# Layer 1's silu written with tanh in a two-layer Mamba and mixture-of-experts kernel

## The chip, the cores and the metric

The kernel runs on one core of a Trainium2 chip. The metric is device microseconds of one execution; lower is better. The core's engines run their own queues in order and meet through semaphores: TensorE (PE; its weight loads are shown apart as PEld), VectorE (DVE), ScalarE (ACT), GpSimd (POOL) and SyncE (SP), which issues most of the DMAs. ACT evaluates its functions (Silu, Tanh, Exp, Ln) with tables; where the next function needs another table, an instruction ACT_TABLE_LOAD stands in its queue.

## The reference

Two layers, each a mixer and a feed-forward, each with a layer norm before it and one behind it, over 4 sequences ("batches") of 512 tokens with 256 features. Layer 0 is a Mamba-2 block with a gated feed-forward, and a routed mixture of 8 experts. The change touches layer 1 alone. Its mixer, for each of 512 inner channels:

```python
projected = jnp.einsum('bld,cd->blc', hidden_states, in_proj_w)
conv_out = _dw_causal_conv_silu(projected, conv_weight, conv_bias)   # 4 taps, then silu
gate = jax.nn.sigmoid(jnp.einsum('bld,cd->blc', hidden_states, gate_proj_w))
X = conv_out.reshape(batch, seqlen, NHEADS, HEADDIM)
dt = jax.nn.softplus(jnp.einsum('blhp,hp->blh', X, dt_w) + dt_b)
a = jnp.exp(dt[..., None] * A)
u = dt[..., None] * B * X
s = _diag_ssm_scan(a, u)          # s_t = a_t s_(t-1) + u_t
y = C * s + D * X
combined = y.reshape(batch, seqlen, INNER) * gate
```

Its mixture of experts: 8 experts with 128 hidden features of which each token uses two, and a shared expert for all.

```python
scores = jax.nn.sigmoid((xt @ gate.T).astype(jnp.float32))
_, sel = jax.lax.top_k(scores + expert_bias[None, :], TOP_K)
...
h = jax.nn.silu(xb @ w1e.T) * (xb @ w3e.T)      # xb: token times its score
oe = (h @ w2e.T).astype(routed.dtype)
...
hs = jax.nn.silu(xt @ shared_w1.T) * (xt @ shared_w3.T)
out = hs @ shared_w2.T
```

## The kernel before

**Two phases.** The first, to about 870 us, runs layer 0's mixer over the four batches and, beside it, the feed-forward and the experts of the batches behind (`feed_forward`, `experts0_in`, `experts0_out`, `experts0_back`). It uses Silu (L601, 8 times), Exp (L708, 64 times), Ln (L212) and, in the feed-forward, Tanh (L310): layer 0's feed-forward already writes silu as `th = tanh(gp / 2)`, then `th = (th + 1) gp` and `hT = 0.5 th up` on DVE (L310 to L313; L1005 to L1007 for the last batch).

The second phase begins with weights loaded on SP's queue (`weight`, L1024: w1i, w1g, dtw, dtb, w1o and more) and constants made on DVE (L1034 to L1041: An = -exp(A_log), BC = B C times a half, D1 = D times a half). Then eight stages run for each batch. Three finish layer 0's experts for two batches; `last_feed_forward` does layer 0's last feed-forward; four are layer 1:

- `mixer1_in`: layer norm, transposition, then for each of four blocks m of 128 channels a projection into a PSUM bank (`ps("b")`, 2 buffers), the convolution (`conv`: one ACT Identity, L199, and three DVE operations, L201, that read the bank) and Silu in place on X (L1058). Then four gates (Tanh, L1065: (1 + tanh) stands for sigmoid, and the constants take up the half), dt from all four X blocks (L1070, with the weights dtw), softplus (`log1p_exp`: Abs L206, Exp L209, Ln L212, with small DVE operations between), and dt, transposed, to DRAM (`by_row`, L255).
- `mixer1_out`: dt comes back from DRAM to all partitions (db, L1088). For each m: POOL makes dt X (L1092), ACT the decay (Exp, L1093) and D1 X (L1094), DVE the scan (L1097), `uu BC + D1 X` (L1098) and the gate (L1099), PE the output projection (L1102); then norm and residual.
- `experts1_in`: layer norm, transposition, router (Tanh, L1139), top two on DVE (L1142 to L1144), scores s (L1146); then the shared expert's hidden features (`gated`: Silu L1116, product L1117).
- `experts1_out`: for each of four chunks c of 128 tokens two halves of four experts each (`inner`). A half's gate and up products (L1164) go to one tile of two PSUM banks (`ps("dc", 2)`, 2 buffers); ACT takes Silu of each expert's 128x128 block with the token's score as scale (L1169, into sg, tag s2b, 2 buffers), DVE makes up times score times sg (L1172), PE turns the result (L1183) and multiplies it by w2 (L1196); then norm, residual and output.

**What sets the order.** Each stage is a generator that yields estimates: PE time, DVE time, a delay, and in some places a stage that has to come first. The loop at the end (L1223 on) picks by these which stage emits its next part, so that stages of different batches stand interleaved in the program. The framework's scheduler then orders each engine's instructions, sets the waits and gives out the buffers; a tile with a tag takes turns in that tag's buffers with all tiles of the tag. `later` pins an instruction to its place in the program.

Of the kernel before, what the change touches and what calls it, by code (L numbers as in the profile page):

```python
# [8 lines left out]
F32 = mybir.dt.float32  # L9
BF16 = mybir.dt.bfloat16  # L10
I32 = mybir.dt.int32
AF = mybir.ActivationFunctionType
ALU = mybir.AluOpType
# [3 lines left out]
B, L, DM = 4, 512, 256  # L17
P = 128
NC = L // P
# [10 lines left out]
OFF, _o = {}, 0  # L30
# [7 lines left out]
def tile_layers(  # L38
# [27 lines left out]
    V, S, G, T = nc.vector, nc.scalar, nc.gpsimd, nc.tensor  # L66
# [4 lines left out]
    small = ctx.enter_context(tc.tile_pool(name="small", bufs=2))  # L71
# [18 lines left out]
    col = base.tile([P, NCOL], F32, tag="col", name="col")  # L90
# [59 lines left out]
    def turned(xT, xn, bank):  # L150
        transposed(xT, [xn[:, c, :] for c in range(NC)], None, bank)
# [364 lines left out]
    with ExitStack() as c1:  # L516
        w0 = c1.enter_context(tc.tile_pool(name="w0", bufs=1))
        wk = c1.enter_context(tc.tile_pool(name="wk0", bufs=1))
# [221 lines left out]
        def batch(b):  # L740
            t = Batch()
            t.b = b
            return t
# [8 lines left out]
        t = batch(0)  # L752
# [39 lines left out]
        for q in range(4):  # L792
            e = q % 2
# [74 lines left out]
        for e in range(2):  # L868
            o = (1 - e) * 64
# [16 lines left out]
        for b in range(B):  # L886
# [71 lines left out]
            for c2 in range(2):  # L958
                p = ps("pj")
                for i in range(2):  # L960
                    c = c2 * 2 + i
# [5 lines left out]
            t = ahead  # L967
# [4 lines left out]
    wk = ctx.enter_context(tc.tile_pool(name="wk2", bufs=1))  # L972
# [56 lines left out]
    dtw = weight(dt_w, "dtw")  # L1029
# [5 lines left out]
    BC = w2.tile([P, 4], F32, tag="BC", name="BC")  # L1035
# [1 line left out]


    D1 = w2.tile([P, 4], F32, tag="D1", name="D1")
    V.tensor_scalar_mul(BC, BC, 0.5)  # L1040
    V.tensor_scalar_mul(D1, col[:, OFF["D1"] : OFF["D1"] + 4], 0.5)  # L1041

    def mixer1_in(b, t):
        xn = wk.tile([P, NC, DM], F32, tag="xn", name="xn", bufs=2)
        layernorm(b, "m", xn)
        yield 0.0, 2.8, 4.0
        xT = wk.tile([P, 2, L], F32, tag="xTb", name="xT1", bufs=1)
        turned(xT, xn, "b")
        yield 1.0, 0.0, 1.8
        t.X = X = wk.tile([P, 4, L], F32, tag="X", name="X", bufs=2)  # L1050
        for m in range(4):
            p = ps("b")
            for k in range(2):
                i = T.matmul(p, w1i[:, k, m * P : (m + 1) * P], xT[:, k, :], start=(k == 0), stop=(k == 1))
                if b + m + k == 0:
                    later(i)
            conv(X[:, m, :], p, lambda t, m=m: cv("cw1", m * 4 + t), cv("cb1", m))
            S.activation(X[:, m, :], X[:, m, :], AF.Silu)  # L1058
            yield 1.72, 2.3, 0.0, (5 if m == 3 else 0)
        t.Gt = Gt = wk.tile([P, 4, L], F32, tag="Gt", name="Gt", bufs=1)  # L1060
        for m in range(4):
            p = ps("b")
            for k in range(2):
                T.matmul(p, w1g[:, k, m * P : (m + 1) * P], xT[:, k, :], start=(k == 0), stop=(k == 1))
            S.activation(Gt[:, m, :], p, AF.Tanh, scale=0.5)  # L1065
            yield 1.72, 0.0, 0.0
        dp = ps("b").rearrange("p (c a h) -> p c a h", a=16, h=8)
        for c in range(NC):
            for m in range(4):
                T.matmul(dp[:, c], X[:, m, c * P : (c + 1) * P], repeated(dtw[:, m, :], 16),  # L1070
                         start=(m == 0), stop=(m == 3))
        dp = dp[:, :, 0, :]
        z = small.tile([P, NC, 8], F32, tag="dtz", name="dtz")
        V.tensor_tensor(z, dp, dtb.unsqueeze(1).to_broadcast([P, NC, 8]), ALU.add)
        dts = small.tile([P, NC, 8], F32, tag="dts", name="dts")
        log1p_exp(dts, small.tile([P, NC, 8], F32, tag="dte", name="dte"), z)
        V.scalar_tensor_tensor(dts, z, 0.0, dts, ALU.max, ALU.add)
        yield 3.44, 1.0, 3.6
        t.dD = by_row(dts, "b", "dD")
        yield 0.5, 0.0, 9.0  # L1080
# [28 lines left out]
    def gated(dst, w1, w3, rhs):  # L1109
        gu = ps("dc", 2)  # L1110
        gp, up = gu[:, :L], gu[:, L:]
        for p, w in ((gp, w1), (up, w3)):
            for k in range(2):
                T.matmul(p, w[:, k, :], rhs[:, k, :], start=(k == 0), stop=(k == 1))  # L1114
        sg = wk.tile([P, L], F32, tag="s2b", name="sg", bufs=2)
        S.activation(sg, gp, AF.Silu)  # L1116
        V.tensor_tensor(dst, sg, up, ALU.mult)  # L1117

    we1 = {}

# [5 lines left out]
    def experts1_in(b, t):  # L1126
        if not we1:
            experts1_weights()
        fg, fb, sw1, sw3 = (we1[n] for n in ("fg", "fb", "sw1", "sw3"))
        xn = wk.tile([P, NC, DM], F32, tag="xn", name="xn", bufs=2)  # L1130
        layernorm(b, "e", xn)
        yield 0.0, 2.8, 4.0
        xT = wk.tile([P, 2, L], F32, tag="xTe", name="xT2", bufs=1)
        turned(xT, xn, "dc")
        t.xb = wk.tile([P, 2, L], BF16, tag="xb", name="xb", bufs=2)
        V.tensor_copy(t.xb, xT)
        yield 1.0, 0.7, 1.8
        sc = small.tile([P, NC, 8], F32, tag="lg1", name="sg")
        S.activation(sc, router(xT, fg, "dc"), AF.Tanh, scale=0.5)  # L1139
        V.tensor_scalar(sc, sc, 0.5, 0.5, ALU.mult, ALU.add)  # L1140
        sel = small.tile([P, NC, 8], F32, tag="sel", name="sel")
        V.tensor_tensor(sel, sc, fb.unsqueeze(1).to_broadcast([P, NC, 8]), ALU.add)  # L1142
        _, o1, _, o2 = top2(sel, small, "e")
        V.tensor_tensor(o1, o1, o2, ALU.add)  # L1144
        t.s = small.tile([P, NC, 8], F32, tag="s1", name="s1")
        V.tensor_tensor(t.s, o1, sc, ALU.mult)  # L1146
        yield 1.8, 4.5, 0.5, 7
        t.hs = wk.tile([P, L], F32, tag="hs", name="hs", bufs=1)
        gated(t.hs, sw1, sw3, xT)
        yield 3.44, 0.7, 0.5  # L1150

    def experts1_out(b, t):

        xb, s, hs = t.xb, t.s, t.hs
        fw1, fw3, fw2, sw2 = (we1[n] for n in ("fw1", "fw3", "fw2", "sw2"))
        hes = {}

        def inner(c):
            hes[c] = he = wk.tile([P, 8, P], BF16, tag="he", name="he", bufs=3)
            for half in range(2):  # L1160
                gu = ps("dc", 2)
                for i, w in enumerate((fw1, fw3)):
                    for k in range(2):
                        T.matmul(gu[:, i * L : (i + 1) * L], xb[:, k, c * P : (c + 1) * P],  # L1164
                                 w[:, half * 4 : half * 4 + 4, k, :], start=(k == 0), stop=(k == 1))
                sg = wk.tile([P, L], F32, tag="s2b", name="sg", bufs=2)
                for i in range(4):
                    e, o = half * 4 + i, i * P
                    S.activation(sg[:, o : o + P], gu[:, o : o + P], AF.Silu, scale=s[:, c, e : e + 1])  # L1169
                for i in range(4):  # L1170
                    e, o = half * 4 + i, i * P
                    V.scalar_tensor_tensor(he[:, e, :], gu[:, L + o : L + o + P], s[:, c, e : e + 1],  # L1172
                                           sg[:, o : o + P], ALU.mult, ALU.mult)
                yield 1.0, 1.0, 1.4

        def outer(c2):

            cs = (2 * c2, 2 * c2 + 1)
            hTs = []
            for c in cs:  # L1180
                p = banks[0].tile([P, 8, P], BF16, tag="b", name="ps_b", bufs=2)
                for e in range(8):
                    T.transpose(p[:, e, :], hes[c][:, e, :], identb)  # L1183
                hT = wk.tile([P, 8, P], BF16, tag="heT", name="heT", bufs=2)
                if c % 2:
                    V.tensor_copy(hT, p)
                else:
                    S.copy(hT, p)
                hTs.append(hT)
            yield 1.6, 0.6, 1.0  # L1190
            p = ps("b")
            outs = [p[:, :DM], p[:, DM:]]
            for c, hT, o in zip(cs, hTs, outs):
                T.matmul(o, hs[:, c * P : (c + 1) * P], sw2, start=True, stop=False)
                for e in range(8):
                    T.matmul(o, hT[:, e, :], fw2[:, e, :], start=False, stop=(e == 7))  # L1196
            add_layernorm(b, outs, "f", last=True, c0=2 * c2)
            nc.sync.dma_start(out=out[b].rearrange("(c p) d -> p c d", p=P)[:, 2 * c2 : 2 * c2 + 2],
                              in_=xs[b][:, 2 * c2 : 2 * c2 + 2])
            yield 2.6, 3.2, 0.0  # L1200

        yield from inner(0)
        yield from inner(1)
        yield from inner(2)
        yield from outer(0)
        yield from inner(3)
        yield from outer(1)
# [134 lines left out]
```

## Time and profile before

Six runs took 1294.72 to 1306.04 us, median 1299.83. The profiled execution:

| | us |
|---|---|
| profiled execution | 1303.15 |
| its span, first to last instruction | 1301.4 |
| first phase | to about 870 |
| end of layer 0's experts beside the first mixers of layer 1 | about 955 to 1096 |
| layer 1 alone | about 1096 to the end |

| window | PE busy | DVE busy | ACT busy | POOL busy |
|---|---|---|---|---|
| 950 to 1100 | 121.2 | 68.2 | 81.2 | 70.6 |
| 1100 to 1200 | 82.5 | 79.1 | 73.2 | 18.8 |
| 1200 to 1301.4 | 72.4 | 64.1 | 52.9 | 11.2 |

A row of a group names line, engine, operation, output<-inputs with shapes, the count, busy time and mean duration of one, and behind the second bar the idle time just before these instructions with what ended it. A row of one line's or one tile's instructions gives the shortest, median and longest duration in ns, and the first and last start. A row of the chain of waits gives start, duration and what it was; one without a tile is an instruction without one, a table load for ACT. A row of waits gives who waited for whom, the total, how often and the longest.

### The profile page before, as it was taken

How to read it: one execution, taken by the hardware profiler on the slowest of the kernel's cores; microseconds unless marked ns; L12 is line 12 of the kernel's file. 1: busy time of each engine (PE TensorE's matmuls, PEld its weight loads, DVE VectorE, ACT ScalarE, POOL GpSimd, SP SyncE). 2: the span in 40 equal slices, each digit the busy share in tenths (PEclk: the TensorE clock that was granted, in tenths of full speed). 3: DMA queues.
4: the chain of work that ended last, by engine and by line, in shares of the span. 5: the costliest groups of instructions: out<-in, count | busy, mean ns of one | idle time of the engine just before them, and what ended most of it. 6: DMA issues, size and time to landing. Idle time of an engine off the chain costs nothing. (4 is left out here: it accounts for less than half of the span.)

```text
span 1301.4 us, 18525 instructions
## 1 busy us (share of the span) xinstructions
PE 1127.3 (87%) x6896; PEld 700.5 (54%) x6896; DVE 795.0 (61%) x1742; ACT 546.4 (42%) x984; POOL 325.3 (25%) x411
## 2 busy tenths in 40 slices
PE   5688988999888999999989999988988697887876
PEld 3344545556545655555545665554666474454543
DVE  5567766656775564677774556754252553966765
ACT  2253442332434334332424443313154556786644
POOL 4021202001214432111133323123143843120100
PEclk9898999999898999999989999998999898999888
DMA  5010100011104443010124441125355552010100
GB/s 154 19 50 17 33 24 29 17 53 33 33 18 135 152 146 118 25 53 18 50 62 126 151 138 57 46 66 175 100 171 190 159 161 78 1 49 1 42 17 25
DMA packets 76153, 97.41 MB, mean 75 GB/s; under 512 B 11008, under 2 KB 62208, under 8 KB 76064
## 3 DMA queue, kind: packets, MB, share of 16 engines
q0 software_dynamic: 13488, 45.10, 11.8%
q1 hardware_dynamic: 53936, 43.26, 11.3%
q10 hardware_dynamic: 8640, 7.87, 1.8%
q8 instruction: 55, 0.90, 0.3%
q14 instruction: 34, 0.28, 0.1%
HBM read 85.25 MB, written 12.12 MB: 75 GB/s over the span
## 5 line engine op out<-in xcount | busy, mean ns | idle before, releaser
L540 PE MATMUL ps_pj<-uT,wg 128*128 128x512 f32 x512 | 261.6, 636 | 12.7 <-ACT bt L698 7.3
L201 DVE SCALAR_TENSOR_TENSOR BT<-ps_pj,col,BT 128x511 f32<-128x511 f32 (+2 forms) x192 | 143.2, 746 | 120.0 <-ACT BT L199 112.6
L719 POOL TENSOR_SCALAR_AFFINE_SELECT sc<-sc 128x1024 f32<-128x1024 f32 x64 | 70.0, 1094 | 475.7 <-DVE sc L716 468.3
L201 DVE SCALAR_TENSOR_TENSOR CT<-ps_pj,col,CT 128x511 f32<-128x511 f32 (+2 forms) x192 | 142.5, 742 | 21.5 <-ACT CT L199 18.8
L540 PEld LDWEIGHTS ps_pj<-uT,wg 128*128 128x128 f32 x512 | 92.2, 198 | 101.4 <-issue 74.9
L199 ACT ACTIVATE CT<-ps_pj,col 128x512 f32<-128x512 f32 x64 | 49.7, 777 | 119.4 <-PE ps_pj L540 119.4
L713 PE MATMUL ps_dc<-CT,BT 64*128 64x128 f32 x1024 | 89.4, 293 | 7.7 <-DVE sc L716 6.0
L713 PEld LDWEIGHTS ps_dc<-CT,BT 64*128 64x128 f32 x1024 | 70.8, 189 | 46.8 <-issue 29.4
L716 DVE TENSOR_TENSOR sc<-sc,ps_dc 128x1024 f32<-128x1024 f32 x64 | 77.6, 1213 | 23.7 <-PE ps_dc L713 21.2
L308 PE MATMUL ps_dc<-vT,wf 128*128 128x512 f32 x192 | 88.0, 597 | 1.8 <-issue 1.1
L199 ACT ACTIVATE BT<-ps_pj,col 128x512 f32<-128x512 f32 x64 | 49.7, 777 | 85.5 <-PE ps_pj L540 85.5
L444 POOL DMA_INDIRECT wx<-in_w_exp_dram,wrow x60 | 59.1, 986 | 92.8 <-PE ps_dc L467 42.3
L708 ACT ACTIVATE sc<-ps_dc 128x1024 f32<-128x1024 f32 x64 | 65.7, 1026 | 39.6 <-PE ps_dc L705 37.9
L467 PE MATMUL ps_dc<-wx,hx 128*128 128x256 f32 x240 | 67.2, 406 | 8.3 <-issue 4.0
L459 PEld LDWEIGHTS ps_dc<-hx,wx 128*128 128x128 f32 x480 | 62.1, 194 | 20.5 <-issue 10.4
L459 PE MATMUL ps_dc<-hx,wx 128*128 128x128 f32 x480 | 66.3, 282 | 6.3 <-DMA wx<-in_w_exp_dram,wrow 4.4
L441 POOL DMA_INDIRECT xr<-XD,token x60 | 58.7, 978 | 42.3 <-PE ps_dc L452 26.6
L698 ACT COPY bt<-ps_pj 128x384 f32<-128x384 f32 x64 | 30.5, 477 | 82.3 <-PE ps_pj L696 75.8
L463 DVE TENSOR_TENSOR hx<-hx 128x256 f32<-128x256 f32 x60 | 28.3, 472 | 60.0 <-ACT hx L462 48.7
L467 PEld LDWEIGHTS ps_dc<-wx,hx 128*128 128x128 f32 x240 | 44.4, 196 | 28.0 <-issue 12.0
L308 PEld LDWEIGHTS ps_dc<-vT,wf 128*128 128x128 f32 x192 | 35.3, 190 | 41.9 <-issue 39.8
L730 PEld LDWEIGHTS ps_pj<-xd,bt 128*128 128x128 f32 x384 | 47.7, 196 | 16.4 <-issue 8.2
(315 smaller groups left out, 2017.7 us busy)
## 6 DMA issues: line engine op xcount, KB each, us to landing
wg<-in_w_in_dram SPq DMA_DIRECT2D x64, 256.0 KB
YS<-yr ACTq DMA_DIRECT2D x60, 128.0 KB
wf<-in_w_gate_dram SPq DMA_DIRECT2D x32, 128.0 KB
wf<-in_w_up_dram SPq DMA_DIRECT2D x32, 128.0 KB
wf<-in_w_down_dram SPq DMA_DIRECT2D x32, 128.0 KB
db<-dD SPq DMA_DIRECT2D x32, 128.0 KB
St<-Mv SPq DMA_DIRECT2D x192, 2.0 KB
x<-in_x_dram SPq DMA_DIRECT2D x4, 512.0 KB
```

Of the source, the lines that this page charges most:

```text
L199: S.activation(dst, p, AF.Identity, bias=bias, scale=w(3))
L201: V.scalar_tensor_tensor(dst[:, s:], p[:, : L - s], w(3 - s), dst[:, s:], ALU.mult, ALU.add)
L308: T.matmul(p, we[:, i * 2 + k, :], vT[:, k, :], start=(k == 0), stop=(k == 1))
L441: keep(G.indirect_dma_start(out=xr[t], out_offset=None, in_=x, in_offset=bass.IndirectOffsetOnAxis(ap=token[:, t : t + 1], axis=0)))
L444: keep(G.indirect_dma_start(out=ws[t], out_offset=None, in_=w_exp, in_offset=bass.IndirectOffsetOnAxis(ap=wrow[:, t : t + 1], axis=0)))
L459: T.matmul(p[:, L + d * P : L + (d + 1) * P], w[:, k * DM + d * P : k * DM + (d + 1) * P], h[:, k * P : (k + 1) * P], start=(k == 0), stop ...
L467: T.matmul(p[:, 2 * P : 2 * P + DM], h[:, (2 + d) * P : (3 + d) * P], w[:, (2 + d) * DM : (3 + d) * DM], start=(d == 0), stop=(d == 1))
L540: T.matmul(p, w[:, k, :], uT[:, k, :], start=(k == 0), stop=(k == 1))
L708: S.activation(sc, df, AF.Exp)
L713: T.matmul(cb[:, e * L + c * P : e * L + (c + 1) * P], of.BT[e * 64 : (e + 1) * 64, c * P : (c + 1) * P], of.CT[e * 64 : (e + 1) * 64, c * ...
L716: V.tensor_tensor(sc, sc, cb, ALU.mult)
L719: G.affine_select(out=scv, in_=scv, compare_op=ALU.is_ge, fill=0.0, base=0, pattern=[[0, 2 * NC], [1, P]], channel_multiplier=-1)
```

## The change

silu(x) = x (1 + tanh(x / 2)) / 2 takes the place of Silu in layer 1, in three spots. In the mixer, X becomes x (1 + tanh(x / 2)), twice silu; BC and D1 get a quarter in place of a half, and dtw is halved once, on DVE. In the shared expert, the factor of a half goes into the last product. In the routed experts ACT takes the tanh of score / 2 times gate; one new DVE operation over the four blocks makes (1 + tanh) times the gate product in PSUM; and the product that follows uses s2 = score squared over two, as one score factor was in Silu's scale before. The router makes both, sh and s2. The tile sc has one buffer in place of two, th1 joins the tag s2b, and two estimates for the planner change.

```diff
     D1 = w2.tile([P, 4], F32, tag="D1", name="D1")
-    V.tensor_scalar_mul(BC, BC, 0.5)
-    V.tensor_scalar_mul(D1, col[:, OFF["D1"] : OFF["D1"] + 4], 0.5)
+    V.tensor_scalar_mul(BC, BC, 0.25)
+    V.tensor_scalar_mul(D1, col[:, OFF["D1"] : OFF["D1"] + 4], 0.25)
+    V.tensor_scalar_mul(dtw, dtw, 0.5)
...
             conv(X[:, m, :], p, lambda t, m=m: cv("cw1", m * 4 + t), cv("cb1", m))
-            S.activation(X[:, m, :], X[:, m, :], AF.Silu)
-            yield 1.72, 2.3, 0.0, (5 if m == 3 else 0)
+            th = wk.tile([P, L], F32, tag="s2b", name="th1", bufs=2)
+            S.activation(th, X[:, m, :], AF.Tanh, scale=0.5)
+            V.scalar_tensor_tensor(X[:, m, :], th, 1.0, X[:, m, :], ALU.add, ALU.mult)
+            yield 1.72, 3.0, 0.0, (5 if m == 3 else 0)
...
         sg = wk.tile([P, L], F32, tag="s2b", name="sg", bufs=2)
-        S.activation(sg, gp, AF.Silu)
-        V.tensor_tensor(dst, sg, up, ALU.mult)
+        S.activation(sg, gp, AF.Tanh, scale=0.5)
+        V.scalar_tensor_tensor(sg, sg, 1.0, gp, ALU.add, ALU.mult)
+        V.scalar_tensor_tensor(dst, sg, 0.5, up, ALU.mult, ALU.mult)
...
-        sc = small.tile([P, NC, 8], F32, tag="lg1", name="sg")
+        sc = small.tile([P, NC, 8], F32, tag="lg1", name="sg", bufs=1)
...
-        t.s = small.tile([P, NC, 8], F32, tag="s1", name="s1")
-        V.tensor_tensor(t.s, o1, sc, ALU.mult)
+
+        t.sh = small.tile([P, NC, 8], F32, tag="s1", name="sh")
+        V.scalar_tensor_tensor(t.sh, o1, 0.5, sc, ALU.mult, ALU.mult)
+        t.s2 = small.tile([P, NC, 8], F32, tag="s2", name="s2")
+        V.scalar_tensor_tensor(t.s2, t.sh, 2.0, t.sh, ALU.mult, ALU.mult)
...
                 for i in range(4):
                     e, o = half * 4 + i, i * P
-                    S.activation(sg[:, o : o + P], gu[:, o : o + P], AF.Silu, scale=s[:, c, e : e + 1])
+                    S.activation(sg[:, o : o + P], gu[:, o : o + P], AF.Tanh, scale=sh[:, c, e : e + 1])
+                V.scalar_tensor_tensor(sg, sg, 1.0, gu[:, :L], ALU.add, ALU.mult)
                 for i in range(4):
                     e, o = half * 4 + i, i * P
-                    V.scalar_tensor_tensor(he[:, e, :], gu[:, L + o : L + o + P], s[:, c, e : e + 1],
+                    V.scalar_tensor_tensor(he[:, e, :], gu[:, L + o : L + o + P], s2[:, c, e : e + 1],
                                            sg[:, o : o + P], ALU.mult, ALU.mult)
-                yield 1.0, 1.0, 1.4
+                yield 1.0, 2.0, 1.4
```

More of the change, by code (lines that the diff above doesn't have):

```diff
@@ L1152, in experts1_out @@
     def experts1_out(b, t):
-        xb, s, hs = t.xb, t.s, t.hs
+        xb, sh, s2, hs = t.xb, t.sh, t.s2, t.hs
         fw1, fw3, fw2, sw2 = (we1[n] for n in ("fw1", "fw3", "fw2", "sw2"))
```

## The prediction

> **What bounds the kernel now.** I read the page's busy shares first. PE is the busiest engine, and ScalarE (ACT), which the change relieves, is the least busy of the three that matter:
>
> ```profile
> PE 1127.3 (87%) x6896; PEld 700.5 (54%) x6896; DVE 795.0 (61%) x1742; ACT 546.4 (42%) x984; POOL 325.3 (25%) x411
> ```
>
> Such shares average over stages, and the changed lines run only in the last quarter, after about 955 us. So the second view is the busy time of each engine in 10 us windows (PE, PEld, DVE, ACT, POOL; instructions in brackets):
>
> ```profile
> 1110.00:1120.00 10.00, 7.05 (x28) 4.34 (x28) 9.86 (x19) 9.90 (x17) 2.55 (x2) 1.00 0.00 0
> 1120.00:1130.00 10.00, 8.74 (x26) 4.21 (x25) 9.86 (x19) 9.85 (x21) 0.00 (x0) 1.00 0.01 2
> 1170.00:1180.00 10.00, 9.91 (x36) 5.54 (x34) 9.56 (x17) 8.55 (x18) 1.24 (x1) 1.00 0.00 1
> 1200.00:1210.00 10.00, 6.66 (x45) 5.15 (x46) 3.14 (x11) 8.26 (x16) 0.00 (x0) 0.66 0.12 27
> ```
>
> The tail repeats a pattern of some 55 us for each batch. There is a burst in which the second mixer of one batch, its successor's input half and the experts of its predecessor run together; in it DVE is full, and ACT as well. Then comes a thin stretch, in which the logarithm of softplus and the trip of dD through DRAM let PE and DVE wait. From 1100 to 1200 us DVE is busy for 79.1 us, from 1200 to 1301 for 64.1.
>
> The third view is ACT's groups from 955 us on. These are the table loads (count, busy us, mean ns):
>
> ```profile
> L1093 ACT ACT_TABLE_LOAD x11 | 14.1, 1283 | 2.4 <-DMA db<-dD 2.2
> L1169 ACT ACT_TABLE_LOAD x8 | 10.3, 1283 | 0.6 <-PE ps_dc L1164 0.5
> L1058 ACT ACT_TABLE_LOAD x6 | 7.7, 1283 | 0.6 <-ACT yr L470 0.4
> L209 ACT ACT_TABLE_LOAD x4 | 5.1, 1283 | 0.1
> L212 ACT ACT_TABLE_LOAD x4 | 5.1, 1283 | 0.1
> L1116 ACT ACT_TABLE_LOAD x3 | 3.8, 1283 | 4.9 <-issue 4.9
> ```
>
> With one each at L422 and L1139 that is 38 loads, 48.8 us. The fourth view is the chain of waits, which shows which of them delay the end:
>
> ```profile
> 1197.99 1.28 ACT L209
> 1199.54 1.28 ACT L1169
> 1201.22 1.28 ACT L212
> 1202.76 1.28 ACT L1169
> ```
>
> Here silu, placed between the Exp and the Ln of one softplus, makes four switches in a row. The chain holds 1.28 us loads at 1115, 1122, 1125, 1143, 1145, 1147 and at these four places, and parts of two more at 1117.84 (0.89) and 1173.06 (0.75).
>
> **What goes.** Without Silu the tail uses Exp, Tanh and Ln. In layer 0 the 24 Tanh of L310 run among the 64 Exp of L708 with one load put down to L310, and the eight of L708 stand against eight for Silu at L601: Exp and Tanh need no switch between them. What remains is Ln and the way back, twice for each of four batches: 8 loads. 30 x 1.283 = 38.5 us leave ACT. Of those on the chain, 1145, 1147, 1201 and 1202 stay (Ln and back); six full ones and two parts go: 6 x 1.28 + 0.89 + 0.75 = 9.3 us. The other 29 us lie where ACT is not what the end waits for.
>
> The load's row ends where the next activation starts (1108.75 plus 1.28, next start 1110.04), and the one before ended 0.02 us ahead: a switch costs 1.3 us here. [...]
>
> **What is added.** All on DVE, priced by the same two operations in layer 0's feed-forward:
>
> ```profile
> L1006 DVE SCALAR_TENSOR_TENSOR hf<-hf,ps_dc x8: 686/687/689, 896.6 to 937.9; 128x512 f32<-128x512 f32 x8
> L1099 DVE SCALAR_TENSOR_TENSOR Gt<-Gt,uu x16: 668/680/694, 1025.8 to 1232.4; 128x512 f32<-128x512 f32 x16
> ```
>
> - X of the second mixer: 16 new (th + 1) X, both inputs in SBUF, 0.68 as L1099: 10.9 us. Lower end 0.67; upper 1.505, the longest L1098, which also reads two SBUF tensors and was stretched beside POOL's uu.
> - Experts: 32 halves, each a new (tanh + 1) gu of 128x512 from PSUM, 0.69: 22.1 us.
> - Shared expert: 4 such, 2.8 us; the last multiply changes form at the same size (L1117 0.68, L1007 0.69).
> - Scores: one 128x32 operation per batch (0.18) and the changed one at the same size. The constants 0.25 and 0.5 replace others. Together under 1 us; the idle DVE of the thin stretches hides them, and uncovered they cost 0.8.
> - The Tanh themselves cost what Silu cost (L1065 0.60 against L1058 0.63).
>
> Sum 35.8 us more on DVE, against 38.5 less on ACT. The two do not cancel, since DVE waits little for ACT: in the waits from 1100 us on,
>
> ```profile
> DVE he L1172 <- ACT sg L1169: 11.4, 14, 1.5
> DVE dts L210 <- ACT dte L209: 6.2, 2, 4.0
> DVE dts L213 <- ACT dts L212: 4.4, 2, 2.8
> ```
>
> and the first of these stays, since Tanh must still come before the product.
>
> [...]
>
> **By stage,** against the profiled execution (1303.15 us, span 1301.4, so 1.75 around it; 3.3 above the median of the runs, to which I carry the difference):
>
> 1. 868 to 876. The new halving of dtw puts a DMA wait on DVE's queue beside L1040 (870.1). dtw is issued at 870.18 behind 1 MB of w1i and w1g; the DMA moved 115, 397, 393 and 284 KB in the microseconds from 870 on, so it lands near 873.7. Behind it stand L325 (872.69) and the stats on which layer 0's last norm waits, and PE idles until ACT's xn at 878. Between 0 (placed behind L325) and 3 us (to 875.7); I take 1.0, an order that places it right behind L1040.
> 2. 955 to 1096. DVE is busy 68.2 of 150 us and has room for 8 X products and one shared expert (6.1 us; uncovered, that is their cost). 11 loads leave ACT, but the chain there holds none; PE waited 3.2 and 0.7 us for ACT's hx copies, some behind loads. Between -5 and 0; I take -2.0.
> 3. 1096 to 1152. DVE has no idle time from 1107 to 1132. Before the last convolution of X releases its PSUM bank to PE it gets three X products (2.0) and three halves less what falls later (1.4); a half on the chain at 1134 and the last X product 1.4. Less the L209 load: 4.8 - 1.3 = +3.5. The ACT loads at 1115 to 1125 are worth nothing, as DVE was full beside them.
> 4. 1152 to 1207. Four X products 2.7, three halves 2.1, a shared expert 0.7, less 2.6 for the loads at 1197.99 and 1199.54: +2.9.
> 5. 1207 to 1272. The chain passes four times from sg over he (1207.9, 1219.6, 1236.9, 1241.1): 4 x 0.69 = 2.8, less 0.3 that L1097 waited for db: +2.5.
> 6. 1272 to the end. Eight halves back to back and no load. Their sg came 1.86 us apart; DVE needs 0.69 + 1.13 for a half and 0.35 for its share of the heT copy, so 2.17: five gaps x 0.31 = 1.6. Then 0.69 for the shared expert on which PE waits, 0.69 in the last half's latency, 0.7 for the norm between: +3.7.
>
> Sum: 1.0 - 2.0 + 3.5 + 2.9 + 2.5 + 3.7 = +11.6, 1299.8 + 11.6 = 1311.4.
>
> **Rivals.**
> - ACT paces the tail, and the order rearranges itself around the freed time: the chain's 9.3 us go, stage 2 gives 5, only the last stage's 3.7 come on top: 1289. For it: ACT full from 1110 to 1130 with loads on the chain. Against: DVE just as full. It decides if the new DVE work slides into the 58 us in which DVE idles after 1100. 0.24.
> - A wash: half of the added work slides so: 1300. 0.13.
> - All DVE work is on the path: th1 of the mixer takes turns with sg in the two buffers of s2b, so ACT's Tanh waits for he of another batch, and DVE's delay comes back to ACT and PE. 35.8 - 9.3 - 2 = +24.5: 1324. For it: both stages stand in the burst. Against: 58 us of idle DVE. It decides once a Tanh of X waits for he in every burst. 0.12.
> - The loads do not go, because Tanh after Ln is given a table without Exp (L1139 had a load of its own at 1094.55, with another for silu right after). Without the load credits: 1.0 + 0 + 4.8 + 5.5 + 2.8 + 3.7 = +17.8, 1318. 0.04.
>
> **How the numbers follow.** My forecast, slower by 12 us, gets 0.47; its own range is 1304 to 1320. A measurement of this kernel tells about 0.5% (6.5 us) from no change: faster is below 1293.3, slower above 1306.3. The first rival gives faster 0.23 and same 0.01; the wash, same 0.13; my forecast's lower edge, same 0.05, the rest slower: 0.23, 0.19, 0.58. The range reaches from 1292 to 1325: it leaves out most of the first rival and the upper edge of the third.
>
> **What would show it.** ACT's table loads after 955 us fall from 38 to about 8, none at L1093 but behind an Ln; DVE's busy time after 1100 rises by about 30 us while ACT's falls by about 20; DVE is full beyond 1132 in the burst; from one half to the next at the end about 2.2 us. If PE's idle time in the bursts shrinks, or the trip of dD comes earlier in each batch, DVE was not the bound and the forecast is wrong; if X's Tanh waits for he, the third rival holds.

## The result and the profile after

Twenty runs of the changed kernel took 1306.12 to 1319.52 us, median 1310.4; the kernel before, 46 runs in all, 1300.06. The ratio is 1.0084 [1.0069, 1.0100]: slower by 10.9 us of 1300. (Here and below, microseconds of a comparison are the ratio less one, times 1300. The chips of the experiments ran the kernel before in 1284 to 1288 us, so only ratios are compared from chip to chip.) The profiled span is 1310.1 us.

Busy time of each engine over the whole span:

```profile
PE 1128.9 (86%) x6896; PEld 699.0 (53%) x6896; DVE 824.7 (63%) x1799; ACT 508.3 (39%) x954; POOL 323.7 (25%) x411
```

ACT lost 38.1 us, DVE gained 29.7. ACT's table loads from 955 us on (count, busy us and mean ns, idle before):

```profile
L212 ACT ACT_TABLE_LOAD x4 | 5.1, 1283 | 0.1
L1176 ACT ACT_TABLE_LOAD x2 | 2.6, 1283 | 1.1 <-PE ps_dc L1171 1.0
L1096 ACT ACT_TABLE_LOAD x1 | 1.3, 1283 | 0.0
L1143 ACT ACT_TABLE_LOAD x1 | 1.3, 1283 | 0.0
```

Eight are left of 38: four for Ln (L212) and four for the way back, wherever the next Tanh or Exp happens to stand. The two large groups of added work on DVE, with the one that follows in each half:

```profile
L1180 DVE SCALAR_TENSOR_TENSOR he<-ps_dc,s,sg 128x128 bf16<-128x128 f32 x128 | 37.8, 340 | 0.4
L1177 DVE SCALAR_TENSOR_TENSOR sg<-sg,ps_dc 128x512 f32<-128x512 f32 x32 | 21.6, 677 | 12.2 <-ACT sg L1176 12.1
...
L1061 DVE SCALAR_TENSOR_TENSOR X<-th,X 128x512 f32<-128x512 f32 x16 | 10.8, 677 | 0.8 <-ACT th L1060 0.6
```

Number and duration are those of the prediction. The time that DVE is covered rises by less than the sum of the rows, as neighbouring rows overlap: four he of 0.340 us take 1.13 us, not 1.36. The 12.1 us of waiting for sg, which stood before he (11.4), now stand before the new product.

The windows of the tail (PE, PEld, DVE, ACT, POOL busy, granted TensorE clock, DMA share, GB/s):

```profile
950.00:1100.00 150.00, 123.20 (x612) 86.68 (x613) 76.88 (x201) 70.37 (x153) 70.36 (x67) 0.91 0.52 152
1100.00:1200.00 100.00, 81.52 (x348) 49.93 (x347) 81.96 (x228) 51.90 (x110) 15.07 (x14) 0.89 0.05 17
1200.00:1310.10 110.10, 77.90 (x391) 46.82 (x388) 79.32 (x251) 46.30 (x127) 11.27 (x12) 0.83 0.08 25
```

From 1100 on ACT has 98.2 us of work (126.1 before, 27.9 less) and DVE 161.3 (143.2 before, 18.1 more).

To compare where the time went, both profiles are laid side by side from one point, the issue of the weights w1i on SP (869.3 before, 863.5 after), and cut at three events: the first uu of batch 2 on POOL, and the writes of dD to DRAM in the third and fourth batch. Us:

| | to uu, batch 2 | to dD, third | to dD, fourth | to the end | sum |
|---|---|---|---|---|---|
| before | 231.0 | 49.2 | 56.1 | 95.8 | 432.1 |
| after | 226.8 | 53.8 | 57.7 | 108.3 | 446.6 |
| predicted difference | -1.0 | +6.4 for both | | +6.2 | +11.6 |
| measured difference | -4.2 | +6.2 for both | | +12.5 | +14.5 |

The first phase was 5.8 us shorter in the after profile though none of its code changed, and single profiles of experiments scatter in the same way: 222 to 232 us in the first column, 223.7 in one that does the work of before (e9 below). The -4.2 can't be put down to the change. Nor can the +6.2 of the two middle columns: e9, with the work of before, takes 111.8 us for them, where the kernel before took 105.3 and the changed one 111.5. The last column can: the same window in both kernels,

```profile
1205.60:1301.40 95.80, 70.12 (x376) 43.87 (x374) 62.83 (x214) 47.36 (x118) 11.24 (x12) 0.87 0.09 28
```

before, and after:

```profile
1201.80:1310.10 108.30, 76.83 (x384) 46.01 (x382) 78.47 (x250) 44.50 (x121) 11.27 (x12) 0.83 0.08 25
```

12.5 us longer, with 15.6 us more on DVE, 6.7 more on PE (at a lower clock, and for 384 rows in place of 376) and 2.9 less on ACT. Of the 36 new expert products 23 stand in it, 21 of halves and 2 of the shared expert, 15.6 us in all. The fourth dD cuts the program at a slightly different place: 21 halves (84 blocks of sg) stand behind it after the change, 19 before. That isn't what makes the stage longer, for e9 has 21 there too, without a new product:

```profile
1183.65:1279.30 95.65, 71.04 (x384) 42.82 (x382) 64.89 (x222) 52.61 (x127) 11.60 (x12) 0.89 0.09 28
```

In every profiled run whose experts get no new product (before, e1, e3, e9, e10, e11) the stage takes 89.1 to 97.9 us; in those with the new product in all batches (after, e2, e4, e7, e8) 107.6 to 111.4.

### The profile page after: what moved, and what is told of

Read it like the earlier page. It is cut to its first block, busy times and chain, and to the rows that moved or that the text cites. A ratio compares the mean times of both kernels' runs of the same rounds, so it can differ in the third digit from the quotient of the medians.

```text
span 1310.1 us, 18525 instructions
## 1 busy us (share of the span) xinstructions
PE 1128.9 (86%) x6896; PEld 699.0 (53%) x6896; DVE 824.7 (63%) x1799; ACT 508.3 (39%) x954; POOL 323.7 (25%) x411
## 5 line engine op out<-in xcount | busy, mean ns | idle before, releaser
L540 PE MATMUL ps_pj<-uT,wg 128*128 128x512 f32 x512 | 258.3, 629 | 13.0 <-ACT bt L698 8.1
L201 DVE SCALAR_TENSOR_TENSOR BT<-ps_pj,col,BT 128x511 f32<-128x511 f32 (+2 forms) x192 | 143.2, 746 | 116.4 <-ACT BT L199 110.6
```

The source lines that it names most:

```text
L201: V.scalar_tensor_tensor(dst[:, s:], p[:, : L - s], w(3 - s), dst[:, s:], ALU.mult, ALU.add)
L540: T.matmul(p, w[:, k, :], uT[:, k, :], start=(k == 0), stop=(k == 1))
```

## The experiments

Each comparison is five rounds against the kernel before on the same chip.

**e1: only the function changes.** In the kernel before, Tanh replaces Silu in all three places; nothing is added, so layer 1 computes another function.

```diff
-            S.activation(X[:, m, :], X[:, m, :], AF.Silu)
+            S.activation(X[:, m, :], X[:, m, :], AF.Tanh)
...
-        S.activation(sg, gp, AF.Silu)
+        S.activation(sg, gp, AF.Tanh)
...
-                    S.activation(sg[:, o : o + P], gu[:, o : o + P], AF.Silu, scale=s[:, c, e : e + 1])
+                    S.activation(sg[:, o : o + P], gu[:, o : o + P], AF.Tanh, scale=s[:, c, e : e + 1])
```

> The kernel before with Tanh in place of Silu in all three spots and nothing else, so that layer 1 computes with tanh(x) where silu(x) belongs: the table loads go, no DVE work comes. Theory (DVE bounds the tail, loads count where the chain holds them): 9 to 14 us below before, 1286 to 1291, with about 8 loads left. Rival (ACT paces the tail): 20 us or more below, under 1280. Rival (loads lie beside full DVE and are worth next to nothing): within 5 us of before.

0.9896 [0.9854, 0.9939], -13.5 us, with 8 loads. The loads do cost time, and the rival in which DVE hides them falls. By themselves they are worth more than the 5.9 us that the prediction's stages credit for them (2.0, 1.3 and 2.6), and about what its first rival gives, 9.3 on the chain and 5 in stage 2.

**e2: only the work on DVE.** The changed kernel with Silu as the function.

```diff
-            S.activation(th, X[:, m, :], AF.Tanh, scale=0.5)
+            S.activation(th, X[:, m, :], AF.Silu, scale=0.5)
...
-        S.activation(sg, gp, AF.Tanh, scale=0.5)
+        S.activation(sg, gp, AF.Silu, scale=0.5)
...
-                    S.activation(sg[:, o : o + P], gu[:, o : o + P], AF.Tanh, scale=sh[:, c, e : e + 1])
+                    S.activation(sg[:, o : o + P], gu[:, o : o + P], AF.Silu, scale=sh[:, c, e : e + 1])
```

> The changed kernel with Silu in place of Tanh in the three spots, so that layer 1 computes with 1 + silu(x / 2) where 1 + tanh(x / 2) belongs: the 36 us of DVE work and the wait for dtw come, the loads stay. Theory: 18 to 24 us above before, 1318 to 1324, so that this and the run without DVE work add up to the change (10). Rival (idle DVE takes half of the work in): 8 to 12 above before. Rival (all of it on the path): 34 or more above.

1.0120 [1.0074, 1.0166], +15.6 us: between the two expectations. With e1 the two parts sum to +2 (about 8 either way), the whole change is +10.9: taken one at a time, each part is partly covered by the other, which the intervals just resolve (8.8 us, 8.4 either way). Going from e2 to the changed kernel, 32 loads are worth some 5 us (6 either way), where e1 found 13.5; going from e1 to the changed kernel, the DVE work costs 24 us, where e2 found 15.6. The last stage of e2,

```profile
1191.50:1302.90 111.40, 78.38 (x384) 45.92 (x382) 78.67 (x250) 55.17 (x129) 12.01 (x12) 0.82 0.08 24
```

has 10.7 us more on ACT than the changed kernel's and the same work on DVE, and is only 3.1 us longer.

**e3 and e4: the two parts.** e3 has the changed mixer alone (Tanh, the product on X, the constants, dtw), e4 the changed experts alone, routed and shared.

```diff
-    V.tensor_scalar_mul(BC, BC, 0.5)
+    V.tensor_scalar_mul(BC, BC, 0.25)
...
+    V.tensor_scalar_mul(dtw, dtw, 0.5)
...
-            S.activation(X[:, m, :], X[:, m, :], AF.Silu)
+            th = wk.tile([P, L], F32, tag="s2b", name="th1", bufs=2)
+            S.activation(th, X[:, m, :], AF.Tanh, scale=0.5)
+            V.scalar_tensor_tensor(X[:, m, :], th, 1.0, X[:, m, :], ALU.add, ALU.mult)
```

> Only the mixer's part of the change: X with Tanh and one more DVE product, constants of a quarter, dtw halved on DVE; the experts keep Silu. Theory: 16 products at 0.68 fall mostly into stages with room or meet loads that go; 0 to 5 us above before. Rival (th1 shares the buffers of sg and holds ACT up): over 8 above.

> Only the experts' part, routed and shared; the mixer keeps Silu in place and dtw is untouched. Theory: 25 us of DVE work, most of it after 1200 where no load stands on the chain: 5 to 10 us above before. If mixer and experts add up to the change, the two parts do not meet; if the experts alone cost as much as the whole change or more, the mixer's part is free.

e3: 0.9993 [0.9964, 1.0021], 23 loads left. e4: 1.0113 [1.0074, 1.0151], +14.7 us, 22 loads left, where 5 to 10 were expected. The mixer's part costs nothing measurable, net of the 15 loads that go with it; the experts' part alone costs as much as the whole change, though 16 loads go with it. So the number of loads does not make the difference between them. That the place of the added work does, and not that of the loads, is not shown by these two runs. e2 speaks for it: all loads stay there, 16 products of X, 13 of the experts' products and the wait for dtw stand ahead of the fourth dD, and it comes 339.9 us behind w1i, for 336.3 before and 335.5 in e9. By these single profiles the added work costs some 4 us up to there and 15.6 behind it. The last stage of e4 has the same DVE work as the changed kernel's:

```profile
1186.40:1297.50 111.10, 76.68 (x379) 45.90 (x377) 78.94 (x246) 44.47 (x121) 11.66 (x12) 0.82 0.08 24
```

**e5: Silu back in the last batch's experts.** In the changed kernel, batch 3's routed and shared experts are as before.

```diff
+        if silu:
+            S.activation(sg, gp, AF.Silu)
+            V.tensor_tensor(dst, sg, up, ALU.mult)
+            return
...
-                    S.activation(sg[:, o : o + P], gu[:, o : o + P], AF.Tanh, scale=sh[:, c, e : e + 1])
-                V.scalar_tensor_tensor(sg, sg, 1.0, gu[:, :L], ALU.add, ALU.mult)
+                    S.activation(sg[:, o : o + P], gu[:, o : o + P], AF.Silu if b == B - 1 else AF.Tanh, scale=sh[:, c, e : e + 1])
+                if b < B - 1:
+                    V.scalar_tensor_tensor(sg, sg, 1.0, gu[:, :L], ALU.add, ALU.mult)
```

> The changed kernel, but the last batch's experts (routed and shared) keep Silu, whose place has no Exp beside it. Theory: 8 products of 0.69 and one of the shared expert leave the last stretch, one or two loads come back; 3 to 6 us below the changed kernel, so 4 to 8 above before. Rival (the loss at the end comes from the batch in front of it): no difference from the changed kernel.

1.0040 [1.0016, 1.0064]: 5.7 us below the changed kernel (3.7 either way), with 9 loads in place of 8. Eight halves and a shared expert give back about half of the loss: 9 products of 0.68 are 6.1 us, so most of their time, by the interval at least a third, was on the path.

**e6: the half's product cut in four.** Each expert's (1 + tanh) gate product of 128 columns by itself, so that the first can start after the first Tanh, for more time on DVE.

```diff
-                V.scalar_tensor_tensor(sg, sg, 1.0, gu[:, :L], ALU.add, ALU.mult)
                 for i in range(4):
                     e, o = half * 4 + i, i * P
+                    V.scalar_tensor_tensor(sg[:, o : o + P], sg[:, o : o + P], 1.0, gu[:, o : o + P], ALU.add, ALU.mult)
```

> The changed kernel with the new product of each half as four products of 128 columns, one behind each Tanh: 4 x 0.28 = 1.13 us of DVE time in place of 0.69 for each of 32 halves, 14 us more on DVE, but the first expert's result 0.8 us sooner. Theory (DVE's throughput is what the added work costs): 8 to 14 us above the changed kernel. Rival (the longer way from Tanh to the released PSUM tile costs it): the same as the changed kernel or below it.

1.0168 [1.0138, 1.0197], 10.9 us above the changed kernel (4.3 either way). The rival, that only the wait for a half's fourth Tanh costs, falls: the earlier start gains less than the added time on DVE takes. The run cannot tell DVE's time from the longer way of a half, as it lengthens both. The last stage:

```profile
1183.30:1304.80 121.50, 84.49 (x384) 49.27 (x382) 84.68 (x314) 44.68 (x121) 11.25 (x12) 0.79 0.07 22
```

DVE has 6.2 us more than in the changed kernel, but the stage is 13.2 us longer, and PE's same 384 products take 7.7 us more at a granted clock of 0.79.

**e7: other work taken off DVE.** The copies of hT behind the odd chunks and of xb go to ACT.

```diff
-        V.tensor_copy(t.xb, xT)
+        S.copy(t.xb, xT)
...
-                if c % 2:
-                    V.tensor_copy(hT, p)
-                else:
-                    S.copy(hT, p)
+                S.copy(hT, p)
```

> The changed kernel with the remaining DVE copies (heT of every second chunk, 8 x 0.69, and the bf16 cast xb, 4 x 0.70) on ACT, which has become idle: 8.3 us less on DVE, 8 x 1.0 and 4 x 1.0 more on ACT. Theory (DVE's throughput): 3 to 7 us below the changed kernel. Rival (latency): the copies take 0.3 us longer each, so the same or above.

1.0081 [1.0049, 1.0112]: 0.4 us below the changed kernel, 5 either way, where 3 to 7 less were expected; the interval does not exclude the lower part of that. The last stage:

```profile
1191.80:1299.40 107.60, 74.90 (x384) 44.90 (x382) 73.84 (x242) 52.43 (x129) 12.89 (x12) 0.85 0.08 25
```

DVE has 4.6 us less and ACT 7.9 more than in the changed kernel, and the stage is 0.7 shorter. This speaks against the amount of DVE work as what sets the stage's length. Together with e5 and e6 it fits that DVE work between a half's Tanh and its he costs the end and DVE work beside it does not. It does not show it: a copy of heT took 1.02 us on ACT in e7, for 0.68 on DVE in the changed kernel, and may cost as much as it spares, and no run took such work off DVE without putting it elsewhere.

**e8: dtw halved on POOL** in the changed kernel, so that no DMA wait stands in DVE's queue.

```diff
-    V.tensor_scalar_mul(dtw, dtw, 0.5)
+    G.tensor_scalar_mul(dtw, dtw, 0.5)
```

> The changed kernel with the halving of dtw on POOL, so that its wait of 3.3 us for the DMA leaves DVE's queue, where the last norm of layer 0 stood behind it. Theory: 1 to 2.5 us below the changed kernel. Rival (PE had other work then): no difference.

1.0077 [1.0050, 1.0104], 0.9 us below the changed kernel with 4 either way: not resolved. The trace shows the step itself. DVE's order of time after the change (start, us, line, operation, idle before it):

```profile
868.59 0.17 DVE L121 TENSOR_SCALAR rsze<-mv 128x4 f32<-128x4 f32 x1
872.10 0.18 DVE L1042 TENSOR_SCALAR dtw<-dtw 128x32 f32<-128x32 f32 x1 [3.34 <-DMA dtw<-in_dt_w_dram]
872.19 0.15 DVE L187 TENSOR_TENSOR off<-mv,rsz 128x4 f32<-128x4 f32 x1
872.27 1.66 DVE L193 SCALAR_TENSOR_TENSOR x<-h,rsz,x 128x256 f32<-128x256 f32 x4
```

and with dtw on POOL:

```profile
853.60 0.17 DVE L121 TENSOR_SCALAR rsze<-mv 128x4 f32<-128x4 f32 x1
854.92 0.16 DVE L187 TENSOR_TENSOR off<-mv,rsz 128x4 f32<-128x4 f32 x1 [1.15 <-POOL rsz L123]
855.00 1.67 DVE L193 SCALAR_TENSOR_TENSOR x<-h,rsz,x 128x256 f32<-128x256 f32 x4
```

and in the kernel before:

```profile
875.81 1.67 DVE L193 SCALAR_TENSOR_TENSOR x<-h,rsz,x 128x256 f32<-128x256 f32 x4
```

So L193 started 6.5 us after w1i's issue before the change (875.81 against 869.33), after the change 8.8 (872.27 against 863.51), with dtw on POOL 6.5 again (855.00 against 848.5). The wait costs 2.3 us at this place.

**e9: the estimates alone.** The kernel before with the two new estimates for the planner.

```diff
-            yield 1.72, 2.3, 0.0, (5 if m == 3 else 0)
+            yield 1.72, 3.0, 0.0, (5 if m == 3 else 0)
...
-                yield 1.0, 1.0, 1.4
+                yield 1.0, 2.0, 1.4
```

> The kernel before with the changed planner estimates alone (3.0 for a block of X, 2.0 for a half): same instructions, another order. Theory (the added work sets the time, not the order): within 4 us of before. Rival (the estimates make the gain of about 4 us that the changed kernel's profile shows up to the second batch's mixer, or part of its loss at the end): more than 5 us off either way.

1.0015 [0.9985, 1.0045]: the order that the estimates bring to the kernel before has no effect that can be told.

**e10, e11, e12: versions.** e10 is e3 with dtw on POOL. e11 has Tanh in the mixer of the first two batches alone, with constants of its own made on POOL, and everything else as before. e12 is the changed kernel with dtw on POOL and Silu in the experts of the last two batches.

```diff
-            S.activation(X[:, m, :], X[:, m, :], AF.Silu)
+            if b < 2:
+                th = wk.tile([P, L], F32, tag="s2b", name="th1", bufs=2)
+                S.activation(th, X[:, m, :], AF.Tanh, scale=0.5)
+                V.scalar_tensor_tensor(X[:, m, :], th, 1.0, X[:, m, :], ALU.add, ALU.mult)
+            else:
+                S.activation(X[:, m, :], X[:, m, :], AF.Silu)
```

> The mixer's part alone with the halving of dtw on POOL. Theory: 1 to 3 us below the mixer's part with it on DVE, so 1 to 4 below before. Rival: no difference from it.

> Tanh in the mixer of the first two batches alone, where DVE has room and loads stand between the copies of layer 0's experts; second constants and the half of dtw made on POOL; all experts keep Silu. Theory: the gain up to the second batch's mixer stays (4 to 6 us) and the later stages are as before: 2 to 6 us below before. Rival (that gain is an accident of order and not of these loads): within 2 us of before or above it.

> The changed kernel with dtw halved on POOL and Silu in the experts of the last two batches, which hold 16 of the 20 halves of the last 100 us. Theory (every half there is on the path with its 0.69): 8 to 12 us below the changed kernel, at before or up to 3 us above it, although loads come back. Rival (the loads that come back cost as much): at the changed kernel less 3 at most.

e10: 0.9980 [0.9963, 0.9997], -2.6 us, the only version with the whole computation whose interval lies below the kernel before, and just so. e11: 0.9983 [0.9963, 1.0004], at the lower edge of what was expected and not told from no change. e12: 1.0019 [0.9995, 1.0043], 8.4 us below the changed kernel (3.7 either way), with 9 loads. It also has dtw on POOL; against e8, which shares that, it is 7.5 us below (4.7 either way). Its last stage:

```profile
1189.80:1290.10 100.30, 74.50 (x384) 45.38 (x382) 66.88 (x230) 45.82 (x122) 11.27 (x12) 0.86 0.09 27
```

Against the changed kernel DVE has 11.6 us less there and the stage is 8.0 us shorter. The experts of the last two batches thus hold most of the loss, by the middle of the intervals, and turning them to Tanh had saved a single load. The trace shows why it is only one: e12 loads for Silu once (L1120, x1), and its other eight loads stand at the same operations as those of the changed kernel (L212 x4, L1184 x2, L1096 and L1147), though in the program the last batch's router takes its Tanh (L1147) between the Silu of two batches. The kernel before shows the same: its 16 Tanh of L1065 run beside the Silu of L1058 with no load put down to them (Silu at 976.66, Tanh at 979.53, Silu at 980.03). Against Exp, Silu did need a switch there (1.28 us at 1103.20, between the Exp of L1093 and the Silu of L1169), against Tanh it did not.

## Why the prediction was right, and where its sum was not

The time and the sign held, 11.6 us slower forecast and 10.9 measured, and so did the main mechanism: the work added on DVE costs more than the loads that leave ACT give back. One term, stage 5, was far too small, and that the total agrees all the same is in part luck. The steps:

- **30 loads go, 8 stay:** as forecast, at 1.283 us. The rival that Tanh after Ln is given another table is out.
- **What the loads are worth:** the sum credits 5.9 us (2.0, 1.3 and 2.6) and takes the loads at 1115 to 1125 for worthless, as DVE was full beside them. Without the new work that is too little: e1 measures 13.5 (7.9 to 19.0). With the new work in place they are worth some 5 by e2 (6 either way), which the 5.9 fits. The work itself has 17.5 us in the sum, and e2 measures 15.6 (6 either way). The timeline of the changed kernel shows no cost of a switch beside its load: the two about one Ln take 1.28 us each, with 0.01 to 0.02 us between the rows:

```profile
1196.90 1.28 ACT L212 ACT_TABLE_LOAD   x1
1198.20 0.23 ACT L212 ACTIVATE dts<-dts 128x32 f32<-128x32 f32 x1
1198.44 1.28 ACT L1176 ACT_TABLE_LOAD   x1
1199.74 1.14 ACT L1176 ACTIVATE sg<-ps_dc,sh 128x128 f32<-128x128 f32 x4
```

- **DVE's price, 35.8 us:** count and durations held (0.677 for the products priced at 0.68 and 0.69). The 16 products of X took 0.656 to 0.693 us, but none of them ran while POOL made a uu, so the upper bound of 1.505 for such a meeting was not tried. A new score operation did meet one twice: sh (L1151), 0.18 us in the last two batches, took 1.28 at 1100.03 and 0.71 at 1165.33, each time to the end of a uu.
- **Stage 1, dtw:** the cost of 1.0 was the wrong reading of right bounds. I put dtw 3.5 us from issue to landing; it took 7.7 (issued at 864.36, used at 872.10). And the halving did not stand right behind L1040 but behind L325 and its statistics, in front of L187 and L193. The step lost 2.3 us.
- **Stage 2, -2.0:** neither shown nor refuted; its window differs by more from run to run.
- **Stages 3 and 4, +6.4:** +6.2 in the one profile, but e9 has +6.5 there with the work of before, so the agreement shows nothing. The chain after the change passes three of the four products of X priced in stage 4 (from 1167.94, 1172.22 and 1180.16, 1.8 us).
- **Stage 5, +2.5:** the term that was mis-sized; it measures +7.8. The step that failed was to count only the four passes of the old chain from sg over he (4 x 0.69). From the fourth dD to the shared expert's activation of the last batch the kernel takes 74.4 us for 66.6 before. That isn't scatter: the other profiled runs without a new product in the experts take 58.8 to 68.7, e2, e4, e7 and e8 74.4 to 77.2. The chain of waits after the change passes there through eight new products, 4.6 us of its time, among them

```profile
1206.89 0.70 DVE sg L1177
1234.70 0.70 DVE sg L1120
1265.33 0.69 DVE sg L1177
```

  The rest of the 7.8 lies in longer waits and slower rows between them and is not attributed.
- **Stage 6, +3.7:** +4.7 from that activation to the end (33.9 us for 29.2); e5, whose last batch has Silu again, takes 29.5 there and still 75.1 in stage 5. The chain passes through three new products, 2.1 us. sg came 2.28 us apart (1278.48 to 1294.42 in seven gaps), forecast 2.17. Of the 23 new products of the whole last stage, 15.6 us, the chain thus holds 11, 6.7 us; the stage grew by 12.5, and e12, which takes 16 halves and two shared experts back, shortens it by 8.0. ACT now waits for DVE there:

```profile
1287.86 1.14 ACT L1176 ACTIVATE sg<-ps_dc,sh 128x128 f32<-128x128 f32 x4 [0.64 <-DVE he L1180]
...
1293.02 1.14 ACT L1176 ACTIVATE sg<-ps_dc,sh 128x128 f32<-128x128 f32 x4 [2.00 <-DVE he L1180]
```

- **DVE as the bound:** right about the experts, too simple as a rule. DVE has idle time in the last stage (78.5 us busy of 108.3), so its total there is not the bound; the way of each half, Tanh, product, four he, release to PE, is the reading that fits e5, e6 and e7 best, though none of them alone shows it. Two of the prediction's signs failed: DVE's work after 1100 rose by 18.1 us where 30 were forecast (ACT's fell by 27.9, forecast 20), and in the burst it was not full, with 8.97, 8.08 and 8.71 us of each 10 from 1110 to 1140. One sign against it came half true: the trip of dD came earlier in the first two batches (1.4 and 9.8 us, counted from w1i), but in e9, which adds no work, too (6.2 and 11.5), and not in the other two.
- **The parts added up:** the expectation of e2 took loads and DVE work as independent. e1 and e2 give +2 together for a measured +10.9, though their intervals are wide (8 either way).
- **Rivals:** ACT pacing the tail (1289) is out by the result, and so is the wash (1300), by the interval. All DVE work on the path (1324) is out as well: its mark was that X's Tanh waits for he, and in the waits after the change X's Tanh waits for X alone. Its buffers do tie ACT to DVE within the experts, in three waits, and to X's product in one short one (from 1100 us on: total, times, longest):

```profile
ACT th L1060 <- DVE X L201: 12.3, 5, 3.4
...
ACT sg L1176 <- DVE he L1180: 8.5, 3, 5.9
...
ACT sg L1176 <- DVE X L1061: 0.4, 1, 0.4
```

So the agreement of 11.6 with 10.9 is in part luck: the profile's last stage cost 6.3 us more than its term, and the span from w1i to the second batch, which the sum had at -1.0, came out 4.2 shorter, within the scatter of the profiles. What the runs attribute is the place: experts +14.7 (5 either way), mixer -0.9 (3.7), both net of the loads that go with them, and last two batches' experts 7.5 (4.7), by e12 against e8.

Open: how the loss of a half splits into DVE's 0.68 us, the later release of the two PSUM banks and the lower clock that PE is granted. No run changed one of these without the others.

## What to carry to other kernels

Judge a table load by the chain: of the 38.5 us that the 30 loads took on ACT the chain held 9.3, and without new work their going gave 13.5 (e1; 7.9 to 19.0). The price of the replacement depends, by these runs, on where it stands: the same (1 + tanh) x product cost nothing measurable in the mixer, net of the loads saved; in the experts, where each half is handed from ACT over DVE to PE, it cost more than half of its duration (e12 against e8: 7.5 us for 18 products of 0.68). Before a function is swapped in every place, count the loads that each place alone would save: the last two batches' experts saved one load for 18 products. And read a chain's handoffs for what they will be after the change, as halves that the chain of before did not pass can become steps of the new one: four were counted in stage 5, eight products stand on the chain after.

## What was not expected of the hardware

PE's granted clock was lower in the longer versions of the last stage: 0.89 in e9, 0.83 after, 0.79 in e6, and PE's busy time for the same 384 rows rose from 71.0 to 76.8 and 84.5 us, with 24.6, 31.5 and 37.0 us idle. It is no rule from these runs: e1 had 0.85 with 24.1 us idle. Within the changed kernel, a half's last four gate and up products (128x512, the trace's rows for L1171) took

```profile
1279.00 1.02 PE L1171 MATMUL ps_dc<-fw,xb 128*128 128x512 bf16 x4 [1.97 <-DVE hs L1121]
1281.63 1.87 PE L1171 MATMUL ps_dc<-fw,xb 128*128 128x512 bf16 x4
...
1286.75 1.02 PE L1171 MATMUL ps_dc<-fw,xb 128*128 128x512 bf16 x4
```

with a granted clock of 1.00 from 1278.9 to 1280.1 and from 1286.7 to 1287.8, and of 0.50 from 1281.6 to 1283.6. Slower products may lengthen the next half in turn, which would fit e6, where 6.2 us more on DVE made the stage 13.2 us longer; that the clock is the cause of this surplus was not tried.
